# Block 1's queries of a fused attention and feed-forward kernel: loaded already turned, where they were normalized and transposed on chip

## The chip, the cores and the metric

The kernel runs on one core of a Trainium2 chip. The metric is the device time of one execution in microseconds (us), the median of three runs: 355.42 us before (355.30 to 355.64). A core has five engines with a queue of their own each, which run in order: TensorE (PE, matrix products; PEld is its weight load), VectorE (DVE), ScalarE (ACT), GpSimd (POOL) and SyncE (SP, which here only starts transfers). GpSimd starts transfers too. The transfers themselves run on 16 DMA engines that all queues share.

## The reference

Eight sequences of 256 tokens with 256 features. One attention step, then one feed-forward network, each behind a layer norm and with a residual:

```python
x = x + xattn(layernorm(x), ctx, ctx, mask)    # causal softmax attention, one head, padded keys masked
x = x + ffn(layernorm(x))

def xattn(query, key, value, mask):
    scores = einsum('bqd,bkd->bqk', query, key) / 16
    scores = where(causal or mask == 0, -inf, scores)
    return einsum('bqk,bkd->bqd', softmax(scores), value)

def ffn(x):                                    # all weights but the scales are -1, 0 or 1
    h = silu((x @ w1.T) * w1_s) * ((x @ w2.T) * w2_s)      # 256 -> 1024
    h = gelu((h @ h1.T) * h1_s)                            # 1024 -> 1024
    h = gelu((h @ h2.T) * h2_s)                            # 1024 -> 1024
    return (h @ w3.T) * w3_s                               # 1024 -> 256
```

## The kernel before

*Tiling.* The 2048 tokens are four blocks (`t` = 0 to 3) of two sequences, 512 tokens each (TB). Features lie on the 128 partitions for the network, tokens for the layer norms. Blocks are worked on in pairs, (0, 1) and then (2, 3): `pair(s, ...)` does the network of a pair, with the two wide layers by a seven-product scheme over 512 by 512 quarters of the weights and sums of quarters.

*Units.* `pair` is a generator that yields after each unit of PE work. In the first pair, units 0 to 7 are the eight gate units of block 0 (`gated`: two groups of four products, `pa` and `pb`, a Silu on ScalarE and a multiplication on VectorE), units 8 to 11 and 12 to 15 are two of the seven products (`px_u`, `p`), and from unit 16 on come the gates of block 1. So block 1's attention must be done before unit 16.

*Attention as stages.* `attention(t, ...)` is a generator too. Its stages are: the queries, scores (`ps`) with mask and maximum, exponentials, transposed probabilities (`pp`, `prt`), product with the values (`pv`) and first residual, statistics, second norm, transposes (`pxt`, `pyt`), casts and rests. Block 0's attention runs whole before everything else. For blocks 1 to 3, `stages_at(t, begin, places...)` writes down by hand behind which unit each stage is issued. Nothing reorders it afterwards: the order of the calls is the order in each engine's queue, and an engine waits at an instruction whose operand isn't there.

*Two ways to queries.* `queries_turned` (blocks 0 and 1, see `near`) takes statistics of x (`sums`: four pairs of bn_stats and bn_aggr on VectorE), normalizes x (`normed`: root on ScalarE, reciprocal and four subtract-and-multiply on VectorE), transposes the result with eight PE products (`pqt`) and copies it to `qt` on ScalarE with the factor 1/16. `queries_loaded` (blocks 2 and 3) loads x already transposed from DRAM into `qt` (SyncE, 512 KB in rows of 2 KB), and sends the means around through DRAM in `on_all`: PE transposes means and variances (`tma`, 8 by 128), VectorE copies that (`hma`), SyncE stores the eight rows to DRAM (L351) and then loads the row of means to all 128 partitions (L355, 256 KB). Two subtractions on VectorE (L397) take the row from `qt`. The factor 1/(16 std) is per token and is multiplied in when the scores are read out (L422), so scores then take two scalar_tensor_tensor operations for each sequence, where queries normalized beforehand take one addition (L419).

*Buffers and queues.* `qt` and the transposed probabilities `prt` share one buffer, tag `qt`. SyncE starts, in this order, block 0's inputs, block 1's inputs xs, kt, mi and vs (512, 512, 256 and 512 KB, issued from 12.82 to 14.21 us), the store of block 0's residual (`kept`, 512 KB, L549, issued at 22.32 us; it is read back much later, in `residual`), then the sums of weight quarters (L670) and block 2's inputs. GpSimd starts the weights: w1 and w2, two quarters `a`, and the quarters `q` that VectorE sums.

Of the kernel before, what the change touches and what calls it, by code (L numbers as in the profile page):

```python
# [67 lines left out]
def network(tc: tile.TileContext, g: Arrays, exact: bool, flag=None):  # L68

    with ExitStack() as ctx:  # L70
        ctx.enter_context(tc.manual_schedule())
        return _network(ctx, tc, g, exact, flag)


def _network(ctx, tc, g, exact, flag):
    nc = tc.nc
# [16 lines left out]
    def new(p, shape, tag, name, dt=F32, **kw):  # L93
        return p.tile(shape, dt, tag=tag, name=f"{v}{name}", **kw)

    def groups(t):

        return ((0,), (1,)) if t == 0 else ((0, 1),)

    def tokens(js):  # L100
        return slice(js[0] * S, (js[-1] + 1) * S)
# [4 lines left out]
    def load_block(t, behind=None):  # L106

        xs = new(io, [P, NT, D], "xs", f"xs_{t}", bufs=2)
        kt = new(io, [P, NB, ND, S], "kt", f"kt_{t}", bufs=2)
        vs = new(io, [P, NT, D], "vs", f"vs_{t}", bufs=2)  # L110
        mi = new(io, [P, TB], "mi", f"mi_{t}", I32)
        span = bass.ts(t, TB)
        if behind is not None:
            for tile_ in (xs[:, 0, :1], kt[:, 0, 0, :1], vs[:, 0, :1], mi[:, :1]):
                behind.memset(tile_, 0)
        step = NT if t else 1
        for i in range(0, NT, step):
            nc.sync.dma_start(out=xs[:, i : i + step, :], in_=g.x[t, :, i : i + step, :])
        for n, js in enumerate(groups(t)):
            own = slice(js[0], js[-1] + 1)  # L120
            nc.sync.dma_start(out=kt[:, own], in_=g.ctx_t[t, :, own])
            if n == 0:
                nc.sync.dma_start(out=mi, in_=g.mask[:, span].to_broadcast([P, TB]))
        nc.sync.dma_start(out=vs, in_=g.ctx_n[t])
        return xs, kt, vs, mi
# [118 lines left out]
    def sums(src, js, mv, name):  # L244

        stats = new(work, [P, NT, nc.vector.BN_STATS_DIM], "stats", f"st{name}", bufs=2)
        for i in range(NT)[tiles(js)]:
            nc.vector.bn_stats(out=stats[:, i, :], in_=src[:, i, :])
            nc.vector.bn_aggr(out=mv[:, :, i], in_=stats[:, i, :])
# [45 lines left out]
    def attention(t, result):  # L295

        made = {}

        def once(tag, name, shape, p=work, **kw):
            if name not in made:  # L300
                made[name] = new(p, shape, tag, f"{name}_{t}", **kw)
            return made[name]

        inputs = loaded.pop(t)
        going = [stages(t, js, once, result, *inputs) for js in groups(t)]
        done = object()
        while going:
            going = [stage for stage in going if next(stage, done) is not done]
            yield
# [6 lines left out]
    def near(t):  # L316

        return exact or t < 2

    def mask_bias(t, js, once, mi):  # L320
        bias = once("bias", "bias", [P, NB, SW])
        if t:
            nc.vector.tensor_scalar(
                bias[:, :, P:], mi.rearrange("p (j k) -> p j k", j=NB), 0.0, NEG, ALU.is_equal, ALU.mult
            )
            parts = bias.rearrange("p j (k n) -> p j k n", k=3)
            nc.vector.tensor_tensor(
                parts[:, :, 0:3:2, :],
                parts[:, :, 1:3, :],
                causal.rearrange("p (j k n) -> p j k n", j=1, k=1).to_broadcast([P, NB, 2, P]),  # L330
                ALU.add,
            )
            return bias
        for j in js:
            k0, k1 = (mi[:, j * S + k * P : j * S + (k + 1) * P] for k in range(2))
            parts = [bias[:, j, k * P : (k + 1) * P] for k in range(3)]
            nc.vector.tensor_scalar(parts[1], k0, 0.0, NEG, ALU.is_equal, ALU.mult)
            nc.gpsimd.tensor_tensor(parts[0], parts[1], causal, ALU.add)
            nc.vector.tensor_scalar(parts[2], k1, 0.0, NEG, ALU.is_equal, ALU.mult)
            nc.gpsimd.tensor_tensor(parts[2], parts[2], causal, ALU.add)  # L340
        return bias

    def on_all(values, tags, name):

        n = values.shape[1]
        turned_ = ps_at.tile([n * NT, P], F32, tag="at", name=f"{v}t{name}")
        nc.tensor.transpose(turned_, values.rearrange("p n i -> p (n i)"), ident)
        here = new(work, [n * NT, P], "here", f"h{name}")
        nc.vector.tensor_copy(here, turned_)
        there = new(rows, [n, TB], "there", name)  # L350
        nc.sync.dma_start(out=there.rearrange("n (i p) -> (n i) p", p=P), in_=here)  # L351
        got = []
        for i, tag in enumerate(tags):
            row = new(work, [P, TB], tag, f"{name}{i}")
            nc.sync.dma_start(out=row, in_=there[i : i + 1].to_broadcast([P, TB]))  # L355
            got.append(row)
        return got
# [19 lines left out]
    def queries_loaded(t, js, once, xs, mi):  # L377


        mva = once("mva", "mva", [P, nc.vector.BN_AGGR_DIM, NT], bufs=2)  # L380
        sums(xs, js, mva, f"a_{t}")
        yield

        std = once("sq", "sda", [P, NT], bufs=2)
        nc.scalar.activation(std, mva[:, 1, :], AF.Sqrt, bias=eps256, scale=256.0)
        yield
        rstd = once("rstd16", "rstd", [P, NT], bufs=2)
        nc.vector.reciprocal(rstd, std)
        qt = once("qt", "qt", [P, ND, TB])
        nc.sync.dma_start(  # L390
            out=qt, in_=g.xt[:, bass.ts(t, TB)].rearrange("(c p) q -> p c q", p=P)
        )
        (mean,) = on_all(mva, ("row",), f"ma_{t}")
        bias = mask_bias(t, js, once, mi)
        yield
        for c in range(ND):
            nc.vector.tensor_tensor(qt[:, c, :], qt[:, c, :], mean, ALU.subtract)  # L397
        yield
        return qt, bias, rstd

    def stages(t, js, once, result, xs, kt, vs, mi):
        cols = tokens(js)
        queries = queries_turned if near(t) else queries_loaded
        qt, bias, factor = yield from queries(t, js, once, xs, mi)
        s = once("y", "s", [P, NB, SW])
        nmax = once("nmax", "nmax", [P, NB, 2])
# [30 lines left out]
        for j in js:  # L437
            for h, (a, e) in enumerate(SPANS):
# [4 lines left out]
                    bias=nmax[:, j, h : h + 1],  # L443
# [47 lines left out]
        xst = once("xst", "xst", [P, ND, TB])  # L491
# [37 lines left out]
        else:  # L529
            std = once("sq", "sdf", [P, NT], bufs=2)  # L530
# [4 lines left out]
            mean, rstd = on_all(mvf, ("row", "row2"), f"mf_{t}")  # L535
# [10 lines left out]
            yield  # L546
            rests(values)
        if js == groups(t)[-1]:
            nc.sync.dma_start(out=kept(t), in_=xst)  # L549
        result[:] = yt  # L550

    stashes: dict = {}

    def kept(t):

        if t not in stashes:
            stashes[t] = new(rows, [P, ND, TB], f"kept{t}", f"kept{t}", bufs=1)
        return stashes[t]
# [451 lines left out]
    def at(s, units, action):  # L1010
        for unit in units if isinstance(units, (tuple, list, range)) else (units,):
            plan.setdefault((s, unit), []).append(action)

    def stages_at(t, first_, *places):
        going = []

        def begin():
            if t not in loaded:
                loaded[t] = load_block(t)
            going.append(attention(t, ready[t]))  # L1020

        at(*first_, begin)
        for s, units in places:
            at(s, units, lambda: next(going[0], None))

    def sums_from(r):
# [3 lines left out]
            homes += [raw[:, j] for j in range(2)]  # L1030
        summing[3 + r] = sum_up(*quarters(3, r, HH // 2, homes))

    stages_at(1, (0, 0), (0, (0, 1, 3, 4, 7, 9, 10, 10, 10, 11, 13, 14)))
    stages_at(
        2, (0, 8), (0, (25, 28, 30, 41, 45, 46, 49, 51, 53, 54, 55, 57, 58, 61, 62, 63))
    )
    stages_at(3, (0, 30), (0, (55, 56, 59, 70, 73, 74, 77)), (1, (1, 4, 8, 10, 11, 13)))
    at(0, (7, 7, 14, 15), lambda: next(summing[2], None))
    at(0, 9, lambda: sums_from(0))
# [74 lines left out]
```

## Time and profile before

| | |
|---|---|
| median of three runs | 355.42 us |
| profiled execution | 355.12 us, its span 353.3 us |
| mean granted TensorE clock | 0.995 |
| gate units 0 to 3 of block 0 | 21.37 to 29.24 us |
| block 1's transposes `pqt` | 29.24 to 30.90 us |
| unit 4 | 30.90 to 32.74 us |
| block 1's scores `ps` | 32.74 to 35.67 us |
| units 5 to 7 | 35.67 to 41.12 us |
| PE idle between 41 and 330 us | 2.7 us |
| HBM read and written | 55.59 and 8.40 MB |

The span runs from the first instruction to the last. The view by waits names what an engine waited for; the chain of waits goes back from the last instruction, at each step to what released it. In the DMA view a queue's row gives packets, MB and the share of the 16 engines' time that its packets took, and a transfer's row its size and the time from issue to landing.

### The profile page before, as it was taken

Reading aid. Unit: us, or ns where it says so; the run is one execution under the profiler, and the core shown is the slowest. Engines: PE = TensorE matmul, PEld = TensorE weight load, DVE = VectorE, ACT = ScalarE, POOL = GpSimd, SP = SyncE. Lnnn points to the kernel's source line nnn. Section 1 sums busy time; section 2 is a strip of 40 time slices with the busy share of each in tenths; the row PEclk is TensorE's granted clock in tenths of the full one; section 3 lists DMA queues with packets and bytes.
Section 4 is the critical chain, followed back from the end, with each engine's and each line's share of the span. In section 5 each row is a group of like instructions: output and inputs, shape, how many; then the busy total and the mean of one; then the engine's idle time right before and its main releaser. Section 6 shows DMA issues by size and latency. Waiting matters only on the chain.

```text
span 353.3 us, 4330 instructions
## 1 busy us (share of the span) xinstructions
PE 340.5 (96%) x1511; PEld 271.2 (77%) x1512; DVE 271.5 (77%) x416; ACT 218.0 (62%) x298; POOL 33.8 (10%) x73
## 2 busy tenths in 40 slices
PE   8799999999999999999999999999999999999993
PEld 3567888778888888887888878777878888888782
DVE  5768966999698938677887687589969899766771
ACT  4558633547946755757772456356896589766730
POOL 1810000210001400022000000000001000000000
PEclk9999999999999999999999999999999999999998
DMA  6699991899495733369518313930564468840032
GB/s 204 234 333 269 268 331 60 269 334 289 137 377 201 238 121 119 130 236 328 190 70 275 115 59 85 360 121 31 224 251 180 160 216 304 291 160 0 0 110 78
DMA packets 20540, 68.54 MB, mean 194 GB/s; under 512 B 2440, under 2 KB 5280, under 8 KB 16928
## 3 DMA queue, kind: packets, MB, share of 16 engines
q0 software_dynamic: 7488, 36.70, 32.3%
q1 hardware_dynamic: 12880, 31.36, 25.9%
q8 instruction: 14, 0.23, 0.3%
q10 hardware_dynamic: 144, 0.13, 0.1%
q14 instruction: 14, 0.11, 0.1%
HBM read 55.59 MB, written 8.40 MB: 181 GB/s over the span
## 4 chain that ended last, share of the span: by engine, by line
PE 68%; DVE 14%; ACT 7%; DMA 4%; issue 4%; POOL 1%; SPq 1%; DVEq 0%; POOLq 0%; ACTq 0%
PE px_u L704 25%; PE px_y L704 15%; PE po L970 8%; PE p L704 5%; PE pa L566 4%; PE pb L566 4%; DMA raw<-h1q 3%; PE pv L470 3%; DVE ol L288 3%; PE ps L411 2%; DVE T L738 2%; ACT oh L687 2%; DMA mi<-mask 1%; DVE seen L199 1%; ACT sign L203 1%
## 5 line engine op out<-in xcount | busy, mean ns | idle before, releaser
L704 PE MATMUL px_u<-ol,a 128*128 128x512 f32 x256 | 72.7, 396 | 0.9 <-DVE ol L288 0.9
L704 PE MATMUL px_u<-oh,a 128*128 128x512 f32 x256 | 73.5, 398 | 0.0
L704 PEld LDWEIGHTS px_u<-ol,a 128*128 128x128 f32 x256 | 48.1, 188 | 12.8 <-DVE ol L288 1.7
L704 PEld LDWEIGHTS px_u<-oh,a 128*128 128x128 f32 x256 | 47.8, 188 | 10.9
L578 ACT ACTIVATE gate<-pa,sc 128x512 f32<-128x512 f32 x32 | 22.0, 690 | 26.2 <-PE pa L566 26.0
L704 PE MATMUL px_y<-oh,a 128*128 128x512 f32 x128 | 35.2, 397 | 0.6 <-ACT nc L732 0.6
L704 PE MATMUL px_y<-ol,a 128*128 128x512 f32 x128 | 34.9, 395 | 0.0
L704 PEld LDWEIGHTS px_y<-oh,a 128*128 128x128 f32 x128 | 23.9, 188 | 6.5 <-ACT nc L732 1.0
L704 PEld LDWEIGHTS px_y<-ol,a 128*128 128x128 f32 x128 | 24.1, 188 | 5.7
L648 POOL DMA_DIRECT2D a<-S x16 | 8.5, 530 | 178.6 <-PE px_u L704 55.6
L203 ACT ACTIVATE sign<-raw 128x1024 bf16<-128x1024 f32 x16 | 16.9, 1054 | 10.6 <-DMA raw<-h1q 6.5
L566 PE MATMUL pa<-hyt,w 128*128 128x512 f32 x64 | 20.6, 403 | 1.4 <-ACT gate L578 0.7
L205 DVE SCALAR_TENSOR_TENSOR sign<-raw,sign 128x1024 bf16<-128x1024 f32 x16 | 19.2, 1219 | 1.9 <-ACT sign L203 1.9
L566 PE MATMUL pb<-hyt,w 128*128 128x512 f32 x64 | 19.9, 391 | 0.3 <-DVE hb L580 0.3
L566 PE MATMUL pa<-lyt,w 128*128 128x512 f32 x64 | 19.9, 392 | 0.0
L566 PE MATMUL pb<-lyt,w 128*128 128x512 f32 x64 | 19.8, 390 | 0.0
L732 ACT ACTIVATE nd<-nd,sc 128x512 f32<-128x512 f32 x16 | 10.7, 717 | 12.2 <-DVE nd L735 12.2
L704 PE MATMUL p<-oh,a 128*128 128x512 f32 x64 | 17.8, 400 | 0.2 <-DVE na L735 0.2
L704 PE MATMUL p<-ol,a 128*128 128x512 f32 x64 | 17.5, 394 | 0.0
L735 DVE TENSOR_TENSOR na<-p,na 128x512 f32<-128x512 f32 x16 | 10.9, 688 | 8.5 <-PE p L704 8.4
L288 DVE TENSOR_TENSOR ol<-nT,oh 128x1024 fp32r<-128x1024 f32 x12 | 14.5, 1221 | 3.8 <-ACT oh L687 3.7
L732 ACT ACTIVATE nb<-nb,sc 128x512 f32<-128x512 f32 x16 | 10.7, 717 | 9.7 <-DVE nb L735 9.7
(168 smaller groups left out, 645.7 us busy)
## 6 DMA issues: line engine op xcount, KB each, us to landing
a<-S POOLq DMA_DIRECT2D x16, 1024.0 KB, 4.7
a<-h1q POOLq DMA_DIRECT2D x6, 1024.0 KB, 7.8
a<-h2q POOLq DMA_DIRECT2D x6, 1024.0 KB, 5.7
raw<-h1q SPq DMA_DIRECT2D x8, 512.0 KB, 4.6
raw<-h2q SPq DMA_DIRECT2D x8, 512.0 KB, 5.4
vs<-ctx_n SPq DMA_DIRECT2D x4, 512.0 KB, 8.1
q<-h1q POOLq DMA_DIRECT2D x4, 512.0 KB, 20.0
q<-h2q POOLq DMA_DIRECT2D x8, 256.0 KB, 14.4
```

The source lines that it names most:

```text
L203: nc.scalar.activation(sign, raw, AF.Sign)
L205: nc.vector.scalar_tensor_tensor(sign, raw, 1.0, sign, ALU.mult, ALU.not_equal, accum_out=count[:, n : n + 1])
L288: nc.vector.tensor_tensor(lo, value, hi.bitcast(F32), ALU.subtract)
L411: nc.tensor.matmul(ps[:, a:e], lhsT=qt[:, c, bass.ts(2 * j + h, P)], rhs=kt[:, j, c, : e - a], start=(c == 0), stop=(c == ND - 1),)
L470: nc.tensor.matmul(pv[:, h, :], lhsT=prt[:, j, bass.ds(a + k * P, P)], rhs=vs[:, 2 * j + k, :], start=(k == 0), stop=(k == n - 1),)
L566: nc.tensor.matmul(pm, lhsT=wc[:, bass.ts(o, P)], rhs=x, start=(n == 0), stop=(n == len(steps) - 1),)
L578: nc.scalar.activation(gate, pa, AF.Silu, scale=sc[:, 0, o : o + 1])
L648: nc.gpsimd.dma_start(out=a, in_=src)
L704: nc.tensor.matmul(bank, lhsT=a[:, k, bass.ts(o, P)], rhs=x[k // 2][part][:, k % 2, :], start=start and (part, k) == steps[0], stop=stop a ...
L732: nc.scalar.activation(out, src, AF.Gelu, scale=sc[:, n, o : o + 1])
L735: nc.vector.tensor_tensor(out, one, other, ALU.add)
L970: nc.tensor.matmul(po, lhsT=w3[j * QK + k][:, bass.ts(o, P)], rhs=xs_[j][k // 2][part][:, k % 2, :], start=(j == 0 and (part, k) == STEPS[0]),
```

## The change

Block 1 now takes `queries_loaded`. In that function, for block 1 alone, the stage after the root has no end of its own, so that root, load, transpose, store and row are issued together, and the reciprocal and the mask's bias come behind the two subtractions instead of ahead of the row. `near`, which chooses the second norm of blocks 0 and 1, stays as it was.

```diff
         std = once("sq", "sda", [P, NT], bufs=2)
         nc.scalar.activation(std, mva[:, 1, :], AF.Sqrt, bias=eps256, scale=256.0)
-        yield
+        if t > 1:
+            yield
         rstd = once("rstd16", "rstd", [P, NT], bufs=2)
-        nc.vector.reciprocal(rstd, std)
+        if t > 1:
+            nc.vector.reciprocal(rstd, std)
         qt = once("qt", "qt", [P, ND, TB])
         nc.sync.dma_start(
             out=qt, in_=g.xt[:, bass.ts(t, TB)].rearrange("(c p) q -> p c q", p=P)
         )
         (mean,) = on_all(mva, ("row",), f"ma_{t}")
-        bias = mask_bias(t, js, once, mi)
+        if t > 1:
+            bias = mask_bias(t, js, once, mi)
         yield
         for c in range(ND):
             nc.vector.tensor_tensor(qt[:, c, :], qt[:, c, :], mean, ALU.subtract)
+        if t == 1:
+
+            nc.vector.reciprocal(rstd, std)
+            bias = mask_bias(t, js, once, mi)
         yield
         return qt, bias, rstd

     def stages(t, js, once, result, xs, kt, vs, mi):
         cols = tokens(js)
-        queries = queries_turned if near(t) else queries_loaded
+        queries = queries_turned if exact or t == 0 else queries_loaded
```

Block 0's store is put in a list and issued behind unit 5:

```diff
         if js == groups(t)[-1]:
-            nc.sync.dma_start(out=kept(t), in_=xst)
+            keep = lambda: nc.sync.dma_start(out=kept(t), in_=xst)
+            if t or exact:
+                keep()
+            else:
+                put_off.append(keep)
         result[:] = yt
+
+    put_off: list = []
```

The stages of block 1 get new places. With no place for the beginning, it is begun at once and its first stage (the statistics) is issued before unit 0:

```diff
-        at(*first_, begin)
+        if first_:
+            at(*first_, begin)
+        else:
+            begin()
+            next(going[0])
         for s, units in places:
             at(s, units, lambda: next(going[0], None))
...
-    stages_at(1, (0, 0), (0, (0, 1, 3, 4, 7, 9, 10, 10, 10, 11, 13, 14)))
+    stages_at(1, None, (0, (1, 6, 7, 8, 9, 10, 10, 10, 11, 13, 14)))
+    at(0, 5, lambda: [store() for store in put_off])
```

So block 1's stages stand: statistics ahead of unit 0 (before: behind unit 0); root, load and row behind unit 1 (root and norm behind 1, transposes behind 3); subtractions, reciprocal and bias behind unit 6; scores behind unit 7 (before: 4); exponentials behind unit 8 (before: 7). From the transposed probabilities behind unit 9 on, the places are the same.

## The prediction

> **What bounds the kernel now.** I read the page first, then the chain of waits between 20 and 60 us, the timeline there, and the DMA view cut into short stretches.
>
> ```profile
> PE 340.5 (96%) x1511; PEld 271.2 (77%) x1512; DVE 271.5 (77%) x416; ACT 218.0 (62%) x298; POOL 33.8 (10%) x73
> DMA  6699991899495733369518313930564468840032
> ...
> 28.33 0.91 PE pb L566 x4
> 29.24 1.66 PE pqt L276 x8
> 30.90 0.92 PE pa L566 x4
> 31.82 0.92 PE pb L566 x4
> 32.74 2.93 PE ps L411 x16
> ...
> 40.21 0.91 PE pb L566 x4
> 41.12 3.73 PE px_u L704 x16
> ```
>
> TensorE (PE) is busy 96% of the span, and from 21.37 us on the chain is almost PE alone: each gate unit (pa and pb of L566) takes 1.82 to 1.83 us, with block 1's eight transposes (pqt) and sixteen score products (ps) between them. PE runs in order, so a removed product is worth its duration and a product whose operand is late stops everything. The second line is the warning: slices 2 to 5 (17.7 to 53 us) have the DMA engines 90% busy or more, and the change puts two dependent transfers there.
>
> ```profile
> mi<-mask SPq DMA_DIRECT2D x1, 256.0 KB, 15.1
> ...
> kept<-xst SPq DMA_DIRECT2D x1, 512.0 KB, 14.2
> ...
> q0 software_dynamic: 149, 0.54, 74.3%
> q1 hardware_dynamic: 152, 0.32, 25.7%
> ...
> q0 software_dynamic: 149, 0.54, 66.7%
> q1 hardware_dynamic: 154, 0.56, 37.7%
> ...
> q0 software_dynamic: 691, 2.03, 108.0%
> ```
>
> These are DMA rows: first the mask row of block 1 (issued at 13.82) and block 0's store (issued at 22.32) with their us to landing, then packets, MB and share of the two queues in 24 to 28, 28 to 32, and 36.6 to 44 us. SyncE's queue (q1) and GpSimd's (q0, the weights) move one packet each in turn, 152 against 149 and 154 against 149, whatever their size. From 12 to 36.6 us q1 moves 720 packets in all. It had been given five transfers (xs, kt, mi, vs of block 1, then the store): 144 each, 128 rows and 16 more. They go in the order of issue: 301 packets are through at 24, 453 at 28, 607 at 32. So vs (packet 576) is through at 28 + (576 - 453)/38.5 = 31.2, the store just before its landing at 36.5.
>
> **The change part by part.**
>
> *PE.* Eight transposes go: -1.66 (chain). One transpose of the means and variances comes; block 2's took 0.27 (below): +0.27. The scores took 2.93 in the chain here and 2.62 and 2.59 for blocks 2 and 3, which are already loaded turned: -0.3. Sum -1.69. With that, unit 3 ends at 29.24 + 0.27 = 29.5 and unit 7 at 29.5 + 4 x 1.82 = 36.8, where PE asks for the scores (before: after unit 4, at 32.74).
>
> *ScalarE and VectorE.* ScalarE loses two copies of 0.60 (qt, L372) and sends its root, with both table loads, 1.4 earlier. VectorE loses four normalizations of 0.41 and gains two subtractions of 0.68 and a copy of 0.25. Neither is on the chain in units 0 to 7; I cost them at nothing. The statistics moved ahead of the first gate take 2.1 (8 instructions from 24.56 to 26.70 before); block 0's last lyt ends at 22.09 and xs has landed at 12.82 + 7.9 = 20.7, so they end at 24.2, and ha_0 moves from 23.89 to 24.2. Its bank is wanted at 26.36: 2 us of cover after its 0.75, and without it the bill would be 0.3.
>
> *The transfers.* The turned queries are one load of 512 KB in rows of 2 KB, 256 + 16 = 272 packets, queued on SyncE behind vs; its buffer is free from about 16 (the last read is the pv product of block 0), long before the ring reaches it. The store no longer stands ahead of it. Then three things follow one another: the store of eight rows of means, the load of one of them to 128 partitions, which waits until that store has landed, and two subtractions. Rows of block 2 and 3 and the two warm-up groups give the prices:
>
> ```profile
> 1.19 4.60 PE L156 MATMUL warm<-zeros 128*128 128x512 bf16 x11 [1.19 <-DVE zeros L159]
> ...
> 18.04 1.67 PE L156 MATMUL warm<-zeros 128*128 128x512 bf16 x7
> ...
> 89.49 0.27 PE L347 MATMUL tma<-ident,mva 128*8 128x128 f32 x1
> ...
> 91.35 0.25 DVE L349 COPY hma<-tma 8x128 f32<-8x128 f32 x1
> 91.63 0.34 SPq L351 DMA_DIRECT2D ma<-hma  x1
> ...
> 92.86 0.35 SPq L355 DMA_DIRECT2D ma<-ma  x1
> ...
> ma<-ma SPq DMA_DIRECT2D x1, 256.0 KB, 6.2
> ...
> ma<-ma SPq DMA_DIRECT2D x1, 256.0 KB, 3.4
> ```
>
> Queries: 31.2 + 272/38.5 = 38.3 through, plus 1.0 to landing (xs and mi landed 0.8 and 1.5 after their last counted packet): 39.3. The means are ready at about 26.8 but their 24 packets stand behind the queries in the same rings: landed about 40.1. Bounds: block 2's row was issued 1.23 after its store with the queue empty, block 3's wait for its store was 2.8. The row then takes 6.2 (block 2, with GpSimd's queue loading beside it) or 3.4 (block 3, quiet); GpSimd's queue is full here to 44 and beyond, so I take 6.2: landed at 46.3. Subtractions of 0.68 end at 47.0 and 47.7; the first score product (0.27) can run between them. PE stands from 36.8 to 47.4, **10.6 us**.
>
> Bounds of that stall. Short: the queries land where the store did (36.5), the means 1.2 later, the row in 3.4 at 41.1, scores from 41.7: 4.9. Long: queries at 40.4, means 2.8, row 7.9 as xs had in the contended stretch: 51.1, first subtraction 51.8: 15.
>
> *What queues behind the wait.* On VectorE the subtractions stand ahead of the reciprocal (0.18), the mask's two operations (0.42 and 0.69) and hb of unit 7 (0.75): these end at 49.7. ScalarE then casts (1.05), loads Exp (1.28) and does the four exponentials (1.86): 53.9. PE meanwhile does scores to 50.0 and two rounds of px_u to 53.7 and waits about 0.3 for the last exponential: +0.3. On SyncE the put-off store stands behind the row; its reader, the residual, is loaded after 158. GpSimd waits for none of this.
>
> *The clock.* The granted clock stands at 1.00 in every slice but the last, but the first eleven 128x512 bf16 products, after PE had stood still, took 0.418 each, and seven of the same at 18 us 0.239. Whether a stop of 10 us brings that back the trace doesn't show (its longest PE stop before 40 us is 1.2). Bounds: 0, and 11 x (0.418 - 0.239) = 2.0. The stop is nearer to the start of the kernel than to any short gap, so I take 2.0.
>
> The Trainium skill has a rule that speaks against this change: "TensorE: Matmul & The Clock Gate", Part 1, says the array falls back to half clock after an idle window of about 3.4 us and needs as long a busy one to leave it. By that page the stop would cost an estimated 3.4 x 0.5 = 1.7, against my 2.0. The page "DMA: Bandwidth & Descriptors" (section on the anatomy of one DMA) would speak the other way: about 2.0 us fixed plus bytes at 436 GB/s makes the three transfers after 31.2 an estimated 3.2 + 2.0 + 2.6, the row at 39.1 and the stop about 3; no transfer of 512 KB in the contended stretch of this trace was near that (7.9, 14.2).
>
> *Sum.* -1.69 + 10.6 + 0.3 + 2.0 = +11.2 on the profiled execution's 355.12 (span 353.30): 366.3. The median of the runs shown, 355.42, is 0.3 higher, so 366.6, which I give as 366.5. After 41 us PE stands still no more than some 2.7 us before its last products, all of it behind VectorE or ScalarE and none behind a transfer, so nothing later gives the stop back.
>
> **The rivals.**
>
> *A short stop.* The queries pass as quickly as the store did, row and store behave as in the quiet, and the clock holds: -1.69 + 4.9 + 0.3 = +3.5, **359**. For it: large weight packets end in before at about 41, and with GpSimd's later small ones (691 packets in 7.4 us) SyncE gets more turns. Against it: the queries have twice the store's packets, and they push GpSimd's end back too.
>
> *The row is in time* (the other side). The whole change then is -1.69: **353.7**. It holds if the row has landed by 36.8 - 1.4 = 35.4, and decides down to a landing at about 37.1, where the stop eats the gain. For it: the queries may be issued at 16 and the means at 27, and transposes, copies and normalizations really go. Against it: SyncE's ring would have to pass 272 + 24 + 144 packets more by then, and by 36.5 it had passed only 144 after vs.
>
> *A long stop*, 15 us with the clock loss: +15.6, **371**.
>
> *The transposes were hidden anyway* and the row is in time, no change: PE has no idle place from 23 to 60 to hide them in, so this is almost nothing.
>
> **How the numbers follow.** Chances: forecast (stop of 7 to 13 us) 0.63, long stop 0.09, short stop 0.16, row in time 0.10, no change 0.02. A measurement here can tell about 0.2% (0.7 us) from no change; so faster 0.10, same 0.02, slower 0.88. The range leaves out the row in time, the shortest stops and the far end of the long one: 358 to 371. The forecast's own range is 362 to 370.
>
> **What would show it.** Right: no pqt of block 1 after 21 us; one tma near 25.5; statistics ending near 24.2; a row of block 1 landing after 40; PE idle before ps with VectorE's subtraction (L400 after) as releaser, and VectorE idle before that behind the transfer; the products after the stop near twice their usual time for some 4 us. Wrong: the row landing before 37, which would mean that SyncE's packets don't queue in order or get more than every second turn; or the stop given back by idle time later.

## The result and the profile after

The changed kernel is slower: 364.7 us (median of six, 363.72 to 365.9) against 355.36, a ratio of 1.0266 with a 95% interval of 1.0248 to 1.0284. The profiled execution took 364.55 us, its span is 362.8 us, 9.5 us longer than before.

The page first: busy time by engine, then PE, the granted clock (PEclk) and the DMA engines in 40 slices of 9.07 us.

```profile
PE 341.7 (94%) x1505; PEld 272.7 (75%) x1505; DVE 271.8 (75%) x417; ACT 217.5 (60%) x296; POOL 33.9 (9%) x73
...
PE   8799099999999999999999999999999999999993
...
PEclk9999769999999999999999999999999999999999
DMA  6799919199769564267835720861376368750032
```

PE has as much work as before (341.7 against 340.5 us) in a longer span. The hole is the 0 in its fifth slice (36.3 to 45.4 us), with the DMA row at 9 above it, and the clock falls to 0.7 and 0.6 there. Both had to be seen together: a stop, and what the stop does to the products after it.

The chain of waits between 25 and 52 us (start, us, what) is the prediction's list of steps, one by one:

```profile
25.57 0.12 PE tma L347
25.70 0.74 DVE ha L593
26.43 0.20 DVE hma L349
26.63 0.02 issue
26.64 11.68 DMA ma<-hma
...
38.39 6.09 DMA ma<-ma
...
44.51 0.70 DVE qt L400
45.21 0.09 issue
45.30 5.62 PE ps L418 x16
50.91 3.86 PE px_u L717 x16
```

The store of 4 KB of means was issued at 26.64 and had landed 11.68 us later. The row took 6.09 more. Before, px_u began at 41.12, now at 50.91. The view of waits (us in total, times, longest) says who stopped whom on PE, and the DMA view of 28 to 32 and 32 to 36 us says why the means were late:

```profile
PE ps L418 <- DVE qt L400: 8.6, 1, 8.6
```

```profile
q0 software_dynamic: 153, 0.56, 68.9%
q1 hardware_dynamic: 154, 0.49, 33.4%
...
q0 software_dynamic: 176, 0.65, 80.2%
q1 hardware_dynamic: 176, 0.36, 26.0%
```

SyncE's queue (q1) moves one packet for one of GpSimd's (q0), 154 to 153 and 176 to 176, and it has 848 to move ahead of the means: four inputs of 144 and the queries' 272. Counted from 16 us, 789 are through at 36.

Last the clock, from the view by windows. The columns are the window, its length, then for PE, its weight loads, VectorE, ScalarE and GpSimd the busy us (and instructions), then the granted clock, the DMA share and GB/s.

```profile
38.00:40.00 2.00, 0.00 (x0) 0.00 (x0) 0.00 (x0) 0.00 (x0) 0.00 (x0) 1.00 1.04 338
40.00:42.00 2.00, 0.00 (x0) 0.00 (x0) 0.00 (x0) 0.00 (x0) 0.00 (x0) 0.71 1.10 219
...
48.00:50.00 2.00, 2.00 (x8) 1.73 (x8) 1.26 (x4) 1.97 (x3) 0.00 (x0) 0.50 0.01 1
50.00:52.00 2.00, 2.00 (x8) 1.61 (x7) 1.05 (x4) 1.05 (x5) 0.00 (x0) 0.73 0.00 0
```

PE stopped at 36.73. The clock fell 4.1 us later, stood at half when the scores began at 45.30, and came back at 51.1. Between 38 and 44 us VectorE, ScalarE and GpSimd do nothing either: what they have left stands behind the subtractions or needs what does.

### The profile page after: what moved, and what is told of

It reads as the page before. It is cut to its first block, busy times and chain, and to the rows that moved or that the text cites. A ratio compares the mean times of both kernels' runs of the same rounds, so it can differ in the third digit from the quotient of the medians.

```text
span 362.8 us, 4323 instructions
## 1 busy us (share of the span) xinstructions
PE 341.7 (94%) x1505; PEld 272.7 (75%) x1505; DVE 271.8 (75%) x417; ACT 217.5 (60%) x296; POOL 33.9 (9%) x73
## 4 chain that ended last, share of the span: by engine, by line
PE 73%; DVE 12%; DMA 6%; ACT 4%; issue 2%; POOL 1%; SPq 1%; DVEq 0%; POOLq 0%; ACTq 0%
PE px_u L717 31%; PE px_y L717 14%; PE po L983 8%; PE p L717 7%; DMA ma<-hma 3%; PE ps L418 3%; PE pb L579 3%; PE pa L579 3%; PE pv L477 3%; DVE ol L288 2%; DVE T L751 2%; DMA ma<-ma 2%; DMA mi<-mask 1%; ACT oh L700 1%; DVE lyt L288 1%
## 5 line engine op out<-in xcount | busy, mean ns | idle before, releaser
L418 PE MATMUL ps<-kt,qt 128*128 128x128 f32 (+1 forms) x64 | 14.1, 384 | 8.6 <-DVE qt L400 8.6
L418 PEld LDWEIGHTS ps<-kt,qt 128*128 128x128 f32 x64 | 11.4, 225 | 10.6 <-issue 9.1
```

Source lines behind the costliest of these rows:

```text
L418: nc.tensor.matmul(ps[:, a:e], lhsT=qt[:, c, bass.ts(2 * j + h, P)], rhs=kt[:, j, c, : e - a], start=(c == 0), stop=(c == ND - 1),)
```

## The experiments

All kernels but one start from the changed kernel. Times are medians, with the ratio to the kernel before on the same chip in the same rounds.

| run | us | ratio, 95% interval | PE stop before the scores, us |
|---|---|---|---|
| changed kernel | 364.7 | 1.0266 (1.0248 to 1.0284) | 8.6 |
| store ahead of the means | 367.36 | 1.0354 (1.0302 to 1.0406) | 10.9 |
| store between means and row | 365.17 | 1.0274 (1.0248 to 1.0300) | 8.8 |
| queries first in the queue | 364.5 | 1.0263 (1.0227 to 1.0300) | 8.2 |
| products of zeros in the stop | 361.98 | 1.0194 (1.0162 to 1.0226) | none, filled |
| queries, keys, mask by ScalarE's queue, unit 5 | 358.51 | 1.0090 (1.0074 to 1.0106) | 3.5 |
| the same, unit 6 | 358.54 | 1.0109 (1.0084 to 1.0133) | 2.9 |
| means and row by ScalarE's queue | 358.32 | 1.0099 (1.0063 to 1.0134) | 2.1 |
| row made by PE | 355.7 | 1.0032 (1.0009 to 1.0056) | 1.2 |
| row made by PE, queries first | 355.09 | 1.0008 (0.9995 to 1.0021) | 0.2 |
| the same, unit 5 | 354.37 | 0.9977 (0.9964 to 0.9990) | none |
| statistics alone, on the kernel before | 354.22 | 0.9971 (0.9960 to 0.9983) | none |
| queries turned on chip, new places | 353.76 | 0.9962 (0.9945 to 0.9979) | none |

**The store ahead of the means.**

```diff
-            if t or exact:
+            if True:
                 keep()
```

> The changed kernel with block 0's store issued at its old place, ahead of the means in SyncE's queue. Theory (the queue passes packets in order, one in turn with the weights' queue): the means wait for 144 packets more at 38 to 44 a us, so the means and everything behind them come 3.3 to 3.8 us later and the time is about 368 us. Rival (the DMA engines are merely full, the place in the queue doesn't matter): 364.7 us, as the changed kernel.

Measured 367.36, 2.7 us above the changed kernel's 364.7 (the two intervals of the ratio are 1.0302 to 1.0406 and 1.0248 to 1.0284, so they do not meet). Its chain shows the same two pieces, the first 2.8 us longer:

```profile
26.36 14.47 DMA ma<-hma
...
40.84 5.70 DMA ma<-ma
...
47.35 5.34 PE ps L418 x16
```

So packets ahead of the means do count, and putting the store off helps the changed kernel. But 144 of them cost 2.8 us, less than the 3.3 to 3.8 that the theory had worked out.

**Queries first.** The queries' load is issued right behind xs, ahead of block 1's kt, mask and vs.

```diff
+    ahead[1] = load_queries(1)     # qt from DRAM, behind xs
+    later.pop()()                  # kt, mask, vs
```

> The changed kernel with block 1's turned queries loaded ahead of its kt, mask and vs in SyncE's queue; means and row stay where they were, behind all four. Theory (the row is what TensorE waits for, and it waits for the number of packets ahead of the means, which is the same): queries land near 27.5, the stop stays near 8.6 us, 364 to 365 us. Rival (the late queries are the cause): the stop is gone, about 354 us.

Measured 364.5: no change. The row of the queries in the DMA view, and the chain at the stop:

```profile
qt<-xt SPq DMA_DIRECT2D x1, 512.0 KB, 11.0
```

```profile
36.52 8.24 issue
44.76 4.93 PE ps L432 x16
```

The queries landed 11.0 us after their issue at 15.58, at 26.6, and the means were as late as ever, since the number of packets ahead of them is the same. The late operand is the row; queries that are early by 12 us buy nothing while it is missing.

**Products of zeros in the stop.**

```diff
+        if t == 1:
+            keep_warm(36)
         return qt, bias, rstd
```

> The changed kernel with 36 products of zeros ahead of block 1's scores, 36 x 0.239 = 8.6 us, as long as TensorE stood still (36.73 to 45.30). They add no work to the result. Theory (the stop has a second price, the clock, which falls to half after it): the granted clock stays at 1.00, the scores take 2.6 instead of 5.6 us, and the time falls by about 3.1 us to 361.6. Rival (the slow scores come from their operands or from waits among them): 364.7 us or more.

Measured 361.98, 2.7 us less than the changed kernel, by adding work. Two windows and the chain of this run:

```profile
36.00:41.00 5.00, 5.00 (x25) 2.22 (x24) 0.92 (x1) 0.36 (x1) 0.00 (x0) 1.00 1.09 303
41.00:46.00 5.00, 4.79 (x24) 2.57 (x22) 2.38 (x6) 0.00 (x0) 0.00 (x0) 1.00 0.95 256
```

```profile
37.55 6.02 DMA ma<-ma
...
43.58 0.04 DVE qt L400
...
44.93 2.66 PE ps L420 x14
47.60 3.73 PE px_u L719 x16
```

The clock stays at 1.00. The row x14 is not all of the scores: two of the sixteen instructions ran from 44.38, and the others waited for the second subtraction. All sixteen, with that wait, take 3.2 us (44.38 to 47.60) where they took 5.6. In the two profiled executions px_u begins 3.3 us apart (47.60 and 50.91): 2.4 of it is the scores, and 0.9 is the row, which landed at 43.57 instead of 44.48 because here the means left 0.3 us earlier and were 0.6 us less on their way. So the second price of the stop is the clock, it is separate from the first, and it is the larger part of this run's gain, not all of it.

**Means and row by ScalarE's queue.**

```diff
-        (mean,) = on_all(mva, ("row",), f"ma_{t}")
+            nc.scalar.dma_start(out=there.rearrange("n (i p) -> (n i) p", p=P), in_=here)
+            yield                                   # row behind unit 2
+            nc.scalar.dma_start(out=mean, in_=there[0:1].to_broadcast([P, TB]))
```

> The changed kernel with the store of the means and the load of their row issued from ScalarE's queue, the row behind unit 2. Theory (they are late because they stand behind the queries in SyncE's queue): the means land within 2 us of 26.6, the row by about 36, and the queries, about 38 to 40, become the last operand; TensorE stands still some 2 to 4 us, too short for the clock to fall much: 357 to 358.5 us. Rival (full DMA engines make the row late on any queue): row near 44, 364.7 us.

Measured 358.32, inside the range of the theory. The row was issued at 31.0, so the means had landed by then (38.3 in the changed kernel), and the queries became the last operand:

```profile
15.75 23.35 DMA qt<-xt
...
40.55 2.66 PE ps L429 x14
```

The trace's releaser for the first subtraction is the queries at 39.1, but the row came at about the same time (8.1 us after its issue), 3 us later than expected. The stop of 2.1 us left the clock alone. The page "DMA: Bandwidth & Descriptors" of the Trainium skill ("Issuing engines are not separate DMA queues") says that starting transfers from another engine only saves the sequencer's time. This run is some 6 us faster than the changed kernel (358.32 against 364.7): another engine's queue also means not standing behind that queue's packets.

**Queries, keys and mask by ScalarE's queue.** Here the means and the row stay on SyncE and have only xs and vs ahead of them; the subtractions stand behind unit 5, in a second run behind unit 6.

```diff
-                nc.sync.dma_start(out=kt[:, own], in_=g.ctx_t[t, :, own])      # block 1
+                nc.scalar.dma_start(out=kt[:, own], in_=g.ctx_t[t, :, own])    # mask and qt alike
-    stages_at(1, None, (0, (1, 6, 7, 8, 9, 10, 10, 10, 11, 13, 14)))
+    stages_at(1, None, (0, (1, 5, 7, 8, 9, 10, 10, 10, 11, 13, 14)))
```

> The changed kernel, means and row through memory on SyncE as changed, but block 1's kt, mask and queries are issued from ScalarE's queue at about 14 to 16 us, so that in SyncE's queue only xs and vs stand ahead of the means, and the subtractions stand behind unit 5. Theory (the loss is the place in the queue alone): the means land by 28.5, the row by 34, queries by about 33; no stop; transposes are gone for 0.12 us of one, so 0.75 us under the run with turned queries at the new places, about 353.0. Rival (a third queue takes turns from the others and row or queries come after 36): 355 to 357 us.

> The same with the subtractions behind unit 6, as the change has them. Theory: the subtractions stand behind a rest on VectorE that ends near 37.0, TensorE asks at 36.7 and waits about 1.1 us: 354 us. Rival (row or queries are later than that anyway): as with unit 5.

Both missed: 358.51 and 358.54, above the rival's range as well. The chain of the first, from an execution of 360.35 us:

```profile
27.04 5.00 DMA ma<-hma
...
32.10 7.72 DMA ma<-ma
...
41.20 4.29 PE ps L432 x14
```

The place in the queue was worth 11.68 - 5.00 = 6.7 us of the means' way, but not all of it, as the theory had claimed. With nothing in front in SyncE's queue, 4 KB still take 5.0 and the row 7.7 while GpSimd's queue, and up to about 32 us ScalarE's, keep the DMA engines full: 12.7 us from 27.0, when PE asks at 37.1 in this run. The clock fell after these stops of 3.5 and 2.9 us too (scores 4.9 and 4.7 us long). The windows of the second run, where the scores begin at 39.79:

```profile
38.00:40.00 2.00, 0.21 (x2) 0.24 (x2) 1.00 (x2) 0.00 (x0) 0.00 (x0) 0.99 1.03 382
40.00:42.00 2.00, 2.00 (x7) 1.60 (x7) 1.97 (x5) 0.00 (x0) 0.00 (x0) 0.50 1.07 287
```

The clock fell only when PE had already begun again.

**The store between means and row.**

```diff
+        if name == "ma_1":
+            put_off.pop()()
         for i, tag in enumerate(tags):
```

> The changed kernel with block 0's store issued between the store of the means and the load of their row, so that SyncE's queue has 144 packets left to move while the means land and the row is issued. In the changed kernel the row was issued at 38.39, and no packet of SyncE's queue moved before 41 us: an empty queue got no turn for some 2.9 us while GpSimd's queue was full. Theory (that wait is of the empty queue, and one that is moving keeps its turn): the store moves in those 3 us, the row follows and lands within 1 us of the changed kernel's 44.5, and the time stays at 364.7 us or within 1 us of it, with 144 packets more in front. Rival (each transfer waits that long, whatever is in front of it, or packets in front simply add): row 3.3 us later, near 367.5 us, as with the store ahead of the means.

Measured 365.17. The row in this run's chain, and SyncE's queue from 41 to 42 us in the changed kernel:

```profile
38.71 5.90 DMA ma<-ma
```

```profile
q1 hardware_dynamic: 7, 0.01, 4.2%
```

The time is the theory's. Its reason is not shown: in the changed kernel SyncE's queue moves no packet from 38.2 to 41.8, here the store's packets fill that hole, and the row starts at about 42 in both, 3.3 to 3.5 us after its issue. Whether the row waits for a start of its own or, here, for the store, can't be told apart; a start of its own would give the same time.

**Queries turned on chip, new places.** The block's queries are made as before; statistics ahead of unit 0, scores behind unit 7, exponentials behind unit 8 and the late store stay as changed.

```diff
-        queries = queries_turned if exact or t == 0 else queries_loaded
+        queries = queries_turned if near(t) else queries_loaded
-    stages_at(1, None, (0, (1, 6, 7, 8, 9, 10, 10, 10, 11, 13, 14)))
+    stages_at(1, None, (0, (1, 3, 7, 8, 9, 10, 10, 10, 11, 13, 14)))
```

> The changed kernel with block 1's queries normalized and transposed on chip again, everything else as changed: statistics ahead of unit 0, scores behind unit 7, exponentials behind unit 8, the store put off. Theory (the whole loss comes from the row's way through memory; places and store cost nothing): within 0.7 us of the kernel before, 355.4. Rival (scores behind unit 7 push VectorE and ScalarE work together and make TensorE wait): 356.5 to 358 us.

It is faster than both kernels, 353.76 against 354.94 for the kernel before, and by more than the theory allowed. The next run takes the kernel before and moves the statistics alone:

```diff
-    stages_at(1, (0, 0), (0, (0, 1, 3, 4, 7, 9, 10, 10, 10, 11, 13, 14)))
+    stages_at(1, None, (0, (1, 3, 4, 7, 9, 10, 10, 10, 11, 13, 14)))
```

> The kernel before with one edit: block 1's statistics ahead of unit 0, all other stages at their old places (scores behind unit 4), queries turned on chip. Theory (half of the 1.66 us of block 1's transposes was a wait for late normalization, since they took 0.87 in the run with new places): transposes take 0.87, and the time is some 0.8 us below before. Rival (the gain of the run with new places came from the later scores): as before, 354.9.

Measured 354.22 against 355.26: -1.0. Its chain, where the kernel before had 1.66 and 2.93:

```profile
28.93 0.87 PE pqt L276 x8
...
31.66 2.62 PE ps L411 x16
```

The transposes' 1.66 was 0.87 of work and 0.79 of waiting for a late normalization, and the scores' extra 0.3 came from late queries too. The statistics alone remove both; the intervals of this run and the one above overlap, so the later scores are not shown to add anything.

**The row made by PE.** Four products of the means, spread over 128 columns, with the identity give the row in PSUM, with no way through memory.

```diff
-        (mean,) = on_all(mva, ("row",), f"ma_{t}")
+            nc.gpsimd.tensor_copy(wide_mean, mva[:, 0, :] ... .to_broadcast([P, NT, P]))
...
+            for i in range(NT):
+                nc.tensor.matmul(mean[:, bass.ts(i, P)], lhsT=wide_mean[:, i, :], rhs=ident,
+                                 start=True, stop=True)
```

> The changed kernel with block 1's row of means made by four TensorE products (means spread over 128 columns by GpSimd, times the identity) in place of the way through memory; the queries are loaded where they were. Theory: the queries, through at about 38.3, are now the last operand; TensorE stands still about 2.5 us, the clock holds, and 355.4 - 1.66 - 0.3 + 0.87 + 2.6 = about 357 us. Rival (the queries' load alone already costs the 8.6 us): 364 us.

> The mean by TensorE and the queries loaded ahead of kt, mask and vs. Theory: queries land near 27.5, keys near 31.5, the mask near 35.5, all before they are asked for; no stop, 355.4 - 1.66 - 0.3 + 0.87 = about 354.3 us, faster than both kernels. Rival (mask or keys, now behind 272 packets more, take the row's place as the late operand): 356 to 359 us.

> The mean by TensorE, queries first in SyncE's queue, and mean products and subtractions behind unit 5 instead of 6. Theory (what was left over there is VectorE's order, the subtractions standing behind a rest of 1.2 us): no wait ahead of the scores, 0.7 us less than behind unit 6, about 354.3, near the run with turned queries at the new places, since the mean products cost TensorE the 0.87 us that the transposes had cost. Rival (the queries or the mask are late): as behind unit 6, 355.1.

Measured 355.7, 355.09 and 354.37. The first shows that the queries, in their old place in the queue, were only 1.2 us late (they landed at 37.8), where 2.5 had been expected. The second missed its 354.3: the first score waited only 0.2 us, but the scores stretched over 3.26 us in the timeline (2.78 with turned queries), because the subtractions stood behind a rest of 1.2 us on VectorE and came in one by one. The third takes that away and lands where it was expected. Its chain says why even the third does not beat turned queries:

```profile
33.23 0.89 PE mean L423 x8
...
37.77 2.62 PE ps L445 x16
```

The trace has two instructions for each of these four products, and they cost PE what eight transposes cost, 0.89 against 0.87.

## Why the prediction was right

366.5 was forecast, 364.7 measured; the mechanism and its place were those forecast. Two sizes were off: the stop was 2.0 us shorter and the clock's price 1.1 us higher than forecast. That they partly cancel is luck, and makes the sum look better than its terms.

*The queue.* The prediction's central step was that the queries' 272 packets and the means behind them pass SyncE's queue one for one with the weights. The trace has that, and the run with the store in front and the run with the queries first confirm that it is the packets ahead of the means that count, wherever the queries stand among them. The step was sized a little too long. I took 38.5 packets a microsecond throughout, and from 32 to 36 us there were 44 (176 in 4 us), so the 848 were through at 37.4, not 38.3; and I took 1.8 us from there to the landing of the means, which took 0.9. They landed at 38.3, not 40.1. The row then took 6.1 (6.2 forecast, from block 2). PE asked at 36.73 (36.8) and stood still until 45.30 (47.4): **8.6 instead of 10.6**. The stop of about 3 us that the working estimated by the Trainium skill's page "DMA: Bandwidth & Descriptors" (section on the anatomy of one DMA) did not come; the page makes that fit for transfers started by GpSimd, and SyncE started these (the three terms also end at 39.0, not 39.1).

*The clock.* Forecast 2.0 as the upper bound of what the warm-up products showed. The scores took 5.62 instead of 2.62 and px_u 3.86 instead of 3.73: **3.1**. The term was mis-sized since I let the slow stretch end as after the start of the kernel, after 4.6 us, while here it lasted from 45.3 to 51.1. It is not one size either: in the three other executions with stops of 8 to 11 us the scores took 4.93, 5.05 and 5.34, a price of 2.3 to 2.7. The Trainium skill's page "TensorE: Matmul & The Clock Gate" (Part 1) has about 3.4 us for either way. Here a stop of 2.9 us was already followed by half clock and one of 2.1 was not; in the four long stops the clock fell 2.1 to 4.1 us after PE had stopped and came back 4.1 to 5.8 us after it had begun again. What sets the moment is not shown.

*What the change removes.* -1.69 held as a sum: the transposes' 1.66 is gone, the single transpose cost 0.12 on the chain, not 0.27. But I read the 1.66 as work, and half of it was a wait. The gain credited to loading the queries was for the larger part a gain of the earlier statistics, which can be had without the load. What loading alone can save of PE's time is 0.87 - 0.12 = 0.75 us. The working knew that the normalization was on VectorE ahead of those products and didn't ask what they waited for; their weight loads had 0.18 to 0.35 us of idle time ahead of them in the timeline, with the normalized tile as releaser. The earlier statistics did cost nothing, as forecast, with less cover than was said: 24.2 + 0.75 leaves 1.4 us to 26.36, not 2, and ha ran at 24.11.

*What queues behind.* The 0.3 forecast for the last exponential did not appear; the transposes of the probabilities take 0.66 on the chain in both kernels. The working had left out the read-out of the scores and its maximum, 1.3 us on VectorE for each sequence, and had let PE run the scores at full clock here. With the slow scores PE asks for the probabilities only at 54.6, and the last exponential ends at 52.9.

*Given back.* Nothing was forecast. The last group of products starts 8.93 us later than before, where px_u had started 9.79 later: 0.86 came back in between, most of it in PE's small waits (0.75 against 1.46 us in the stretch from 210 to 260 us, 200 to 250 before). The end of the span, after the last product, took 0.6 more.

*The rivals.* The short stop was 359: three runs that use ScalarE's queue came to its number (358.3 to 358.5), with shorter stops than its 4.9 us and, in two of them, a lost clock; the change itself didn't. The row in time did not happen in any run that sends it through memory. A version in which the queue is clear was expected to gain the forecast's -1.7 and something more; in the run that came nearest to it memory's two trips took 12.7 us, and only 10 were there. Issuing the queries behind the row, or the scores behind a later unit, was not tried.

## What to carry to other kernels

Before a value is sent through memory, count the packets already ahead of it in that queue and the turns that the other queues take; the time is that count over the rate, with a start of some 3 us for each trip that finds its queue empty in such a stretch, and the bytes say little (4 KB took 5.0 us, 256 KB 5.7 to 8.1). A stop of PE (of 2.9 us and more here) is to be priced with the clock that falls after it. And before a group of products is priced for removal, split it into work and wait: here moving the statistics ahead, the cheapest part of the change, was worth 1.0 us alone, and with the queries still turned on chip the changed order reached 353.76 us, the lowest median of all runs, though the intervals don't tell it from the statistics alone.

## What had not been expected of the hardware

A transfer of 4 KB took 11.68 us from issue to landing behind other transfers, and 5.00 us with none left in front of it in its queue, while other queues kept the DMA engines full. After the row was issued at 38.39, SyncE's queue moved nothing until 41.8 us; block 1's xs, issued at 12.82 in the kernel before, shows the same: its first packets move after 16.2 us. So do the row with the store ahead (issued at 40.84, first packet at 44.2), means and row with the keys on ScalarE's queue (27.04 and 30.4, 32.10 and 35.4) and, on ScalarE's own queue, means and row (26.57 and 29.8, 30.98 and 34.4). So each dependent trip pays 3.2 to 3.6 us before its first packet in such a stretch, on top of the moving, and the 12.7 us of two trips are for more than half such starts. In the quiet, block 2's means, issued at 91.63 in the kernel before, moved at 92.2. Why the start takes so long was not tried.

Products that do nothing made the kernel 2.7 us faster, for the larger part by keeping the clock at 1.00 through a stop.
